# Strassen products of the GRU gates: the second and third of each seven added by TensorE in the PSUM bank of the first and fifth

## The chip, the cores and the metric

The kernel runs on one core of a Trainium2 chip. The metric is the device time of one launch in microseconds (us), as the median of the runs shown. TensorE (PE in the profile, with its weight loads listed apart as PEld), VectorE (DVE), ScalarE (ACT), GpSimd (POOL) and SyncE (SP) each run their own instructions in order and wait for each other by semaphores.

## The reference, cut to what matters

The first layer is a gated recurrent unit (GRU) over 128 graphs of 128 nodes and 256 channels. Its inputs are the normalised rows `h`, a convolution branch `x_conv` and a neighbour sum `x_nmp`; the change touches the gates only:

```python
x_in = jnp.concatenate([x_conv, x_nmp], axis=-1)
gi = x_in @ w_ih.T + b_ih
gh = x @ w_hh.T + b_hh
r = jax.nn.sigmoid(gi_r + gh_r)
z = jax.nn.sigmoid(gi_z + gh_z)
nn_ = jnp.tanh(gi_n + r * gh_n)
return (1.0 - z) * nn_ + z * x
```

Around it stand a layer norm with ReLU ahead of each layer and residual additions. The second layer is a grouped graph convolution on the first 25 nodes of each graph.

## The kernel before, in words

Everything is float32. The graphs are taken in 32 groups `q` of four. Two early stages (`stage_a`, `stage_b`, for two batches) do the convolution through a Fourier transform; `early(q)` computes the neighbour sums. The third stage begins at 720.4 us of the profiled execution. It runs `stage_c(q)` for every group, and beside it the second layer: `rows(q)` normalises the 32 rows that a group hands over, `prepare(blk)` and `block(blk)` work on 16 graphs at once.

The order of all instructions is made when the kernel is built, by `Order.run`. Each lane is a list of generators. A step of a generator ends with `yield cost, delay`: the cost is TensorE time, and is added to a clock; the generator may go on when the clock has passed its due time (the clock plus the delay). Among lanes that are due, the one with the least cost so far, divided by its weight, goes first. The lane of `stage_c` holds two groups at a time (`ahead=2`), and takes the one with the earlier due time. The lane of the second layer has weight 0.2, so it waits until the groups are not due, that is, at the yields with a delay of 0.2 between the products with `wn`.

In `stage_c(q)` three gate matrices are multiplied by Strassen's scheme, as seven products each over 2 x 2 blocks: `wrz` (reset gate `r` and update gate `z`, two output blocks of 128, six matmuls for each product), `wh` (one matmul for each) and `wn` (two). The operands are `hT`, `xm` and `xc`, and their block sums `th`, `tm` and `tc`, which DVE makes (`sums`, `some_sums`, line 552). With product indices 0 to 6 for the scheme's P1, P2, P3, P4, P5, P6, P7, an index below 3 uses a block of the plain operand and the others use a sum. A matmul of 128 x 256 appears in the profile as two records. Every product gets a PSUM bank from a pool: `pgat` has three banks (the products of `wrz` and `wn`), `ptmp` five (all else). A freed bank is handed out again in the order in which its last reader stands in the program; the next writer waits for that reader.

The order around the change, in a group: two products of the inverse transform (`pi`, line 673); the parts of products 0, 1 and 2 of `wrz` that need `hT` and `xm` only; in between `turn_back` (eight transposes `pc`, DVE line 690 and ACT line 693 make `xc`); then the parts that need `xc`. ACT copies product 0 to `u2` (line 740), DVE adds product 1 to it into `r1` (line 741), ACT copies product 2 to `r2` (line 745). DVE then builds the sums `u2`, `u3` for the other outputs (lines 761, 762, 769, 779, 780, 788), in the same way for `wh` in `va`, `vb`, `vt` (lines 760 to 797), and for `wn` in `r` itself (lines 805 to 823). Then come Tanh (line 825), three POOL operations for each half (lines 828 to 831, `d` and `z`), and, 11.0 of the builder's clock later, the eight transposes `po` (line 848) of the group before. The tiles `d` of a group's end have the same slots as `u2` and `u3` of the next group.

Of the kernel before, what the change touches and what calls it, by code (L numbers as in the profile page):

```python
# [10 lines left out]
AF = mybir.ActivationFunctionType  # L11
ALU = mybir.AluOpType
# [195 lines left out]
def kernel(ctx: ExitStack, tc: tile.TileContext, x, adj, consts, vecs, w_se, conv1_w,  # L208
                    conv2_w, w_msg, b_msg, w_ih, w_hh, W1, W2, b2, fusion_w, out):
    nc = tc.nc  # L210
# [7 lines left out]
    ptmp = ctx.enter_context(tc.tile_pool(name="ptmp", bufs=5, space=PSUM))  # L218
# [18 lines left out]
    def v(name, i=None):  # L237
        a, b = VAT[name]
        return vec[:, a:b] if i is None else vec[:, a + i:a + i + 1]
# [306 lines left out]
    def sums(name, q, x):  # L546


        t = LATE["co"].tile([P, 4, D], FP, tag=name, name=f"{name}{q}", bufs=1 + (name != "tc"))
        operands = ((0, x[:, 0, D:], x[:, 0, :D]), (1, x[:, 1, D:], t[:, 0]),  # L550
                    (2, x[:, 1, D:], x[:, 0, D:]), (3, t[:, 1], x[:, 1, :D]))
        return t, [lambda i=i, a=a, b=b: nc.vector.tensor_sub(t[:, i], a, b)  # L552
                   for i, a, b in operands]

    def some_sums(q, n):

        if q in IN:
            if q not in SUMS:
                hT, xm = IN[q]
                (th, a), (tm, b) = sums("th", q, hT), sums("tm", q, xm)  # L560
                SUMS[q] = th, tm, a + b
            while SUMS[q][2] and n != 0:
                SUMS[q][2].pop(0)()
                n = n and n - 1
# [92 lines left out]
    def stage_c(q):  # L657
# [11 lines left out]
        for h in range(2):  # L669
            yt = IN2.pop((q, h))  # L670
            pi = ptmp.tile([P, 2, D], FP, tag="tmp", name=f"pi{q}_{h}")
            for b in range(2):
                nc.tensor.matmul(pi[b * 64:(b + 1) * 64], inv[:F], yt[:, b::2],  # L673
                                 start=True, stop=True)
# [5 lines left out]
        def turn_back():  # L680

            for h in range(2):
                s = slice(h * D, (h + 1) * D)
                pc = ptmp.tile([P, 2, D], FP, tag="tmp", name=f"pc{q}_{h}")
                for co in range(2):
                    for i in range(2):
                        nc.tensor.transpose(pc[:, co, i * P:(i + 1) * P],  # L687
                                            xi[:, 2 * h + i, co * P:(co + 1) * P], ident)
                for co in range(2):
                    nc.vector.scalar_tensor_tensor(xc[:, co, s], pc[:, co],  # L690
                                                   scl["bn2"][:, co:co + 1], hT[:, co, s],
                                                   op0=ALU.mult, op1=ALU.add)
                    nc.scalar.activation(xc[:, co, s], xc[:, co, s], AF.Relu,
                                         bias=sft["bn2"][:, co:co + 1])

        wrz, wn, wh = LATE["wrz"], LATE["wn"], LATE["wh"]

        def factor(i, x, t):

            return ((x[:, 0, :D], x[:, 1, :D], x[:, 1, D:])[i] if i < 3  # L700
                    else t[:, (3, 0, 1, 2)[i - 3]])

        def part(ps, w, i, xs, first, last):


            n = [(m, o) for o in xs for m in range(w.shape[3] // P)]
            for j, (m, (k, x, t)) in enumerate(n):
                nc.tensor.matmul(ps[:, m], w[:, i, k, m * P:(m + 1) * P], factor(i, x, t),  # L708
                                 start=first and j == 0, stop=last and j == len(n) - 1)

        def product(w, i, xs, pool=pgat):
            ps = bank(w, i, pool)
            part(ps, w, i, xs, True, True)
            return ps

        def bank(w, i, pool=pgat):
            return pool.tile([P, w.shape[3] // P, D], FP, tag="gat" if pool is pgat else "tmp",
                             name=f"p{w.shape[3]}{q}_{i}")

        def sigmoid(dst, src, b):  # L720
            for m in range(2):
                nc.scalar.activation(dst[:, m], src[:, m], AF.Sigmoid, bias=brz[:, b + m:b + m + 1])  # L722

        xs = [(0, hT, None), (2, xm, None), (1, xc, None)]
        r = fr.tile([P, 2, 512], FP, tag="r", name=f"r{q}")
        u2 = fr.tile([P, 2, D], FP, tag="u2", name=f"u2{q}")
        u3 = fr.tile([P, 2, D], FP, tag="u3", name=f"u3{q}")
        r1, r2 = r[:, :, :D], r[:, :, D:]  # L730
        ps = [bank(wrz, i) for i in range(3)]
        for i in range(3):
            part(ps[i], wrz, i, xs[:2], True, False)
            yield 1.75, 0.0
            if i == 0:
                turn_back()
                yield 0.9, 0.0
        for i in range(2):
            part(ps[i], wrz, i, xs[2:], False, True)
        nc.scalar.activation(u2, ps[0], AF.Copy)  # L740
        nc.vector.tensor_tensor(r1, u2, ps[1], ALU.add)
        sigmoid(r1, r1, 0)
        yield 1.75, 0.0
        part(ps[2], wrz, 2, xs[2:], False, True)
        nc.scalar.activation(r2, ps[2], AF.Copy)
        tcs, todo = sums("tc", q, xc)
        for operation in todo:
            operation()
# [1 line left out]
        xs, xh = [(0, hT, th), (2, xm, tm), (1, xc, tcs)], [(0, hT, th)]  # L750

        ve = fr.tile([P, 3, 1, D], FP, tag="ve", name=f"ve{q}")
        va, vb, vt = ve[:, 0], ve[:, 1], ve[:, 2]
        r11, r12, r21, r22 = r[:, 0:1, :D], r[:, 0:1, D:], r[:, 1:2, :D], r[:, 1:2, D:]

        def gate(dst, src, row):
            nc.vector.scalar_tensor_tensor(dst, src, v("b_hh", 4 + row), dst,
                                           op0=ALU.add, op1=ALU.mult)

        nc.scalar.activation(va, product(wh, 0, xh, ptmp), AF.Copy)  # L760
        nc.vector.tensor_tensor(u2, u2, product(wrz, 5, xs), ALU.add)
        nc.vector.tensor_add(r2, r2, u2)
        yield 3.03, 0.0
        nc.vector.tensor_tensor(vt, va, product(wh, 1, xh, ptmp), ALU.add)
        gate(r11, vt, 0)
        nc.vector.tensor_tensor(va, va, product(wh, 5, xh, ptmp), ALU.add)
        yield 0.87, 0.0
        p5 = product(wrz, 4, xs)
        nc.vector.tensor_tensor(r2, r2, p5, ALU.add)  # L769
        sigmoid(r2, r2, 0)  # L770
        some_sums(q + 1, 2)
        yield 2.6, 0.0
        nc.vector.tensor_tensor(vb, va, product(wh, 6, xh, ptmp), ALU.add)
        yield 0.43, 0.0
        while q and q - 1 not in C_DONE:
            yield 0.0, 0.5
        z = fr.tile([P, 2, 512], FP, tag="z", name=f"z{q}")
# [1 line left out]
        nc.vector.tensor_tensor(u3, u2, product(wrz, 6, xs), ALU.add)  # L779
        nc.vector.tensor_tensor(z2, u3, p5, ALU.add)  # L780
        sigmoid(z2, z2, 2)
        some_sums(q + 1, 2)
        nc.vector.tensor_tensor(vt, vb, product(wh, 3, xh, ptmp), ALU.add)
        gate(r21, vt, 1)
        yield 3.03, 0.0
        xt = fr.tile([P, 4, D], FP, tag="xt", name=f"xt{q}")
        load_x(xt, q)
        nc.vector.tensor_tensor(z1, u3, product(wrz, 3, xs), ALU.add)
        sigmoid(z1, z1, 2)
        some_sums(q + 1, 2)  # L790
        yield 2.6, 0.0
        h5 = product(wh, 4, xh, ptmp)
        nc.vector.tensor_tensor(vb, vb, h5, ALU.add)
        gate(r22, vb, 1)
        nc.vector.tensor_tensor(va, va, h5, ALU.add)  # L795
        nc.vector.tensor_tensor(va, va, product(wh, 2, xh, ptmp), ALU.add)
        gate(r12, va, 0)
        some_sums(q + 1, 2)
        yield 0.87, 0.0

        xs = [(1, xm, tm), (0, xc, tcs)]
        u2 = fr.tile([P, 2, D], FP, tag="u2", name=f"v2{q}")
        u3 = fr.tile([P, 1, D], FP, tag="u3", name=f"v3{q}")
        v1, v2 = u2[:, 0:1], u2[:, 1:2]
        nc.scalar.activation(v1, product(wn, 0, xs), AF.Copy)
        yield 0.87, 0.2
        nc.vector.tensor_tensor(v2, v1, product(wn, 5, xs), ALU.add)
        nc.vector.tensor_add(r12, r12, v2)
        yield 0.87, 0.2
        p5 = product(wn, 4, xs)  # L810
        nc.vector.tensor_tensor(r12, r12, p5, ALU.add)
        yield 0.87, 0.2
        nc.vector.tensor_tensor(u3, v2, product(wn, 6, xs), ALU.add)
        nc.vector.tensor_add(r22, r22, u3)
        nc.vector.tensor_tensor(r22, r22, p5, ALU.add)
        nc.vector.tensor_add(r21, r21, u3)
        nc.vector.tensor_add(r11, r11, v1)
        yield 0.87, 0.2
        nc.vector.tensor_tensor(r21, r21, product(wn, 3, xs), ALU.add)
        yield 0.87, 0.2  # L820
        nc.vector.tensor_tensor(r11, r11, product(wn, 1, xs), ALU.add)
        yield 0.87, 0.2
        nc.vector.tensor_tensor(r12, r12, product(wn, 2, xs), ALU.add)
        for dc in (1, 0):
            nc.scalar.activation(r[:, dc], r[:, dc], AF.Tanh, bias=v("b_ih", 4 + dc))  # L825

# [276 lines left out]
    for bat, (during_a, during_b) in enumerate(((0.66, 0.5), (0.2, 0.65))):  # L1103
# [12 lines left out]
        tc.tile_pool(name="co", bufs=1, side="right", reuse_waits="tile"))  # L1116
    loads = Lane([stage_n(q) for q in range(NQ)])
    groups = Lane([stage_c(q) for q in range(NQ)], ahead=2)
    second = [setup_1()] + [part(blk) for blk in range(NBLK) for part in (prepare, block)]
    beside.weight = 0.5  # L1120
# [43 lines left out]
```

## Time and profile before

| | |
|---|---|
| median of 5 runs | 2127.11 us (2125.21 to 2132.17) |
| the profiled execution's own time | 2127.27 us |
| its span, first to last instruction | 2125.5 us |
| PE busy | 2052.5 us (97%) |
| DVE busy | 1240.2 us (58%), 2999 instructions |
| ACT busy | 699.9 us (33%) |
| POOL busy | 724.1 us (34%) |
| third stage, 720.4 to 2030.0 us | 1309.60 us, PE busy 1289.57, DVE 798.71, ACT 411.05 |

Durations of single instructions are means over their group in the profile. A record of a matmul ends when its result is modelled to be complete, so neighbouring records overlap; the distance from start to start is what a matmul takes from the engine. Idle time of PE is time in which no record is open.

### The profile page before, as it was taken

The page shows a single profiled execution, that of the slowest core. Times are in us where ns is not written, and L with a number is a line of the kernel's source. Part 1 is how long each engine was busy: PE and PEld are TensorE (multiplying, and loading weights), DVE is VectorE, ACT ScalarE, POOL GpSimd, SP SyncE. Part 2 cuts the span into 40 slices and gives each one's busy share as a digit, 9 for nine tenths or more (in the row PEclk, how much of TensorE's full clock was granted, in tenths as well). Part 3 has the DMA queues.
Part 4 walks back from the last instruction along what each step waited for, and adds up shares of the span by engine and source line. Part 5 has one row for each costly group of instructions (what it writes and reads, how often), then busy time and mean ns, then how long its engine had stood idle before and what let it go on. Part 6 is the DMA issues. An engine that isn't in the chain of part 4 may idle for free.

```text
span 2125.5 us, 31227 instructions
## 1 busy us (share of the span) xinstructions
PE 2052.5 (97%) x11316; PEld 1664.8 (78%) x11316; DVE 1240.2 (58%) x2999; ACT 699.9 (33%) x1575; POOL 724.1 (34%) x900
## 2 busy tenths in 40 slices
PE   6999999999999999999999999999999999999998
PEld 4667888788888777788778878878887887878875
DVE  5665444776544566756654655675565655665642
ACT  3554222344222343323233332233233223323333
POOL 2443665231566123512323233223323323233230
PEclk9999999999999999999999999999999999999999
DMA  9997778744777534222223222223232233223121
GB/s 179 267 266 231 259 256 264 207 142 148 260 259 257 180 109 153 67 92 61 76 70 102 77 79 84 77 75 85 71 99 73 78 92 91 78 80 101 26 78 50
DMA packets 187052, 281.68 MB, mean 133 GB/s; under 512 B 20685, under 2 KB 140242, under 8 KB 186898
## 3 DMA queue, kind: packets, MB, share of 16 engines
q1 hardware_dynamic: 156066, 184.81, 30.5%
q0 software_dynamic: 30000, 94.13, 13.9%
q8 instruction: 90, 1.47, 0.3%
q10 hardware_dynamic: 832, 0.74, 0.2%
q14 instruction: 64, 0.52, 0.1%
HBM read 187.34 MB, written 92.27 MB: 132 GB/s over the span
## 4 chain that ended last, share of the span: by engine, by line
PE 83%; DVE 8%; DMA 4%; ACT 1%; issue 1%; POOL 1%; SPq 0%; ACTq 0%; DVEq 0%; POOLq 0%
PE p L708 36%; PE pa L501 7%; PE pm L600 5%; PE ph L1024 5%; PE pz L1033 5%; PE pc L397 4%; PE pb L501 3%; PE pi L673 3%; PE px L626 3%; PE pf L408 2%; DMA wfd<-ws 2%; PE pg L1067 1%; PE po L848 1%; PE pc L687 1%; PE py L1007 1%
## 5 line engine op out<-in xcount | busy, mean ns | idle before, releaser
L828 POOL TENSOR_TENSOR d<-hTc,r 128x512 f32<-128x512 f32 x64 | 82.3, 1286 | 318.7 <-ACT r L825 308.3
L857 POOL DMA_DIRECT2D out<-xt x128 | 71.8, 567 | 263.1 <-DVE xt L854 259.0
L501 PE MATMUL pa<-wf,X 128*128 128x256 f32 x640 | 152.4, 381 | 0.0
L524 DVE SCALAR_TENSOR_TENSOR y<-pa,kk 128x512 f32<-128x512 f32 x78 | 53.8, 690 | 147.4 <-ACT kk L523 147.4
L722 ACT ACTIVATE r<-r,brz 128x256 f32<-128x256 f32 x128 | 58.1, 500 | 226.2 <-DVE r L769 198.5
L708 PE MATMUL p<-th,wrz 128*128 128x256 f32 x512 | 131.5, 379 | 0.7 <-ACT u L740 0.7
L708 PE MATMUL p<-tc,wrz 128*128 128x256 f32 x512 | 131.5, 379 | 0.4 <-DVE tc L552 0.4
L708 PE MATMUL p<-tm,wrz 128*128 128x256 f32 x512 | 131.4, 379 | 0.0
L501 PEld LDWEIGHTS pa<-wf,X 128*128 128x128 f32 x640 | 118.1, 190 | 16.4 <-issue 2.2
L397 PE MATMUL pc<-c1w,hTa 128*128 128x256 f32 x512 | 123.2, 387 | 3.7 <-ACT ef L588 2.3
L600 PE MATMUL pm<-wmsg,hT 128*128 128x256 f32 x512 | 123.9, 388 | 0.0
L690 DVE SCALAR_TENSOR_TENSOR xc<-pc,s_bn,hTc 128x256 f32<-128x256 f32 x128 | 53.1, 477 | 115.6 <-PE pc L687 115.6
L1024 PE MATMUL ph<-yz,w 128*128 128x96 f32 (+3 forms) x640 | 114.8, 334 | 4.0 <-DVE ve L795 2.7
L1024 PEld LDWEIGHTS ph<-yz,w 128*128 128x128 f32 x640 | 92.7, 202 | 26.0 <-issue 14.9
L397 PEld LDWEIGHTS pc<-c1w,hTa 128*128 128x128 f32 x512 | 94.4, 192 | 22.0 <-DVE h L400 4.0
L600 PEld LDWEIGHTS pm<-wmsg,hT 128*128 128x128 f32 x512 | 97.6, 194 | 16.5 <-issue 1.8
L1033 PE MATMUL pz<-hh,w 128*128 128x96 f32 (+3 forms) x640 | 108.5, 322 | 0.8 <-ACT hh L1026 0.8
L708 PEld LDWEIGHTS p<-th,wrz 128*128 128x128 f32 x512 | 97.2, 190 | 14.3 <-ACT u L740 1.1
L708 PEld LDWEIGHTS p<-tc,wrz 128*128 128x128 f32 x512 | 97.2, 190 | 14.0 <-DVE tc L552 0.8
L708 PEld LDWEIGHTS p<-tm,wrz 128*128 128x128 f32 x512 | 97.3, 190 | 13.2
L722 ACT ACTIVATE z<-z,brz 128x256 f32<-128x256 f32 x128 | 58.1, 501 | 145.8 <-DVE z L780 90.9
L1033 PEld LDWEIGHTS pz<-hh,w 128*128 128x128 f32 x640 | 87.2, 192 | 19.3 <-ACT hh L1026 1.5
(209 smaller groups left out, 4669.2 us busy)
## 6 DMA issues: line engine op xcount, KB each, us to landing
wf<-wfd SPq DMA_DIRECT2D x160, 256.0 KB, 3.6
wfd<-ws POOLq DMA_DIRECT2D x64, 320.0 KB, 7.2
yd<-y POOLq DMA_DIRECT2D x80, 256.0 KB, 3.5
yt<-yd SPq DMA_DIRECT2D x64, 320.0 KB, 4.5
w<-in_W SPq DMA_DIRECT2D x40, 512.0 KB, 3.6
xa<-in_x SPq DMA_DIRECT2D x128, 128.0 KB, 5.3
hTd<-hTa POOLq DMA_DIRECT2D x32, 512.0 KB, 4.6
hT<-hTd SPq DMA_DIRECT2D x32, 512.0 KB
```

What stands on the lines that cost most here:

```text
L397: nc.tensor.matmul(pc[:, i], hT[:, k, (2 * h + i) * N:(2 * h + i + 1) * N], c1w[:, k], start=(k == 0), stop=(k == 1))
L501: nc.tensor.matmul(ps, xk(k), WF[f][:, k, s], start=(k == 0), stop=(k == 1))
L524: nc.vector.scalar_tensor_tensor(y, pa, 2.0, kk[:, None].to_broadcast([P, 2, D]), op0=ALU.mult, op1=ALU.subtract)
L600: nc.tensor.matmul(pm[:, i], hT[:, k, j * N:(j + 1) * N], LATE["wmsg"][:, k], start=(k == 0), stop=(k == 1))
L626: nc.tensor.matmul(px[:, dc, i], msgs[h][:, i, dc * P:(dc + 1) * P], aT[:, 2 * h + i], start=True, stop=True)
L673: nc.tensor.matmul(pi[b * 64:(b + 1) * 64], inv[:F], yt[:, b::2], start=True, stop=True)
L708: nc.tensor.matmul(ps[:, m], w[:, i, k, m * P:(m + 1) * P], factor(i, x, t), start=first and j == 0, stop=last and j == len(n) - 1)
L722: nc.scalar.activation(dst[:, m], src[:, m], AF.Sigmoid, bias=brz[:, b + m:b + m + 1])
L828: nc.gpsimd.tensor_sub(d, hT[:, dc], r[:, dc])
L857: nc.gpsimd.dma_start(out=out[q * GB + j, WIDE:].rearrange("(t n) c -> n t c", n=WIDE), in_=xt[j * WIDE:(j + 1) * WIDE, 1:4])
L1024: nc.tensor.matmul(ph, w1[:, k, m * P:(m + 1) * P], yz[:, k, :, o:o + n], start=(k == 0), stop=(k == 1))
L1033: nc.tensor.matmul(pz, w2[:, g, m, cc * P:(cc + 1) * P], hs[g][:, m], start=(m == 0), stop=(m == 3))
```

## The change

The weights and the 63 matmuls of a group stay. What changes is where they add up, and when:

- The parts that need `hT` and `xm` only are now those of products 0, 5 and 4 of `wrz` (banks `p1`, `p6`, `p5`), not 0, 1 and 2.
- Product 1 of `wrz` is added by TensorE into bank `p1` after ACT has copied product 0 out of it to `u2`; the sigmoid of `r1` reads the bank. Product 2 is added into `p5` after DVE has read product 4 from it for `z2`; one DVE addition then gives `r2`. The copy of line 745 goes.
- The same for `wh` (product 1 into `h1` after the copy to `va`, product 2 into `h5` after DVE's addition to `vb`) and for `wn` (product 1 into `n1` after the copy to `v1`, product 2 into the bank of product 4).
- Two products of `wh` and two of `wn` and `wrz` no longer ask for a bank. The additions to `r12` and `r22` become one of twice the width.
- The order of the products, of the additions of the next group's sums and of some yields changes with it. `skip_group_check` is an argument for the builder's check of groups alone.

```diff
-        def part(ps, w, i, xs, first, last):
+        def part(ps, w, i, xs, first, last, again=False):
...
                                  start=first and j == 0, stop=last and j == len(n) - 1,
+                                 skip_group_check=again)
...
-        ps = [bank(wrz, i) for i in range(3)]
-        for i in range(3):
-            part(ps[i], wrz, i, xs[:2], True, False)
+        early = [(0, hT, th), (2, xm, tm)]
+        p1, p6, p5 = bank(wrz, 0), bank(wrz, 5), bank(wrz, 4)
+        for ps, i in ((p1, 0), (p6, 5), (p5, 4)):
+            part(ps, wrz, i, early, True, False)
             yield 1.75, 0.0
             if i == 0:
                 turn_back()
                 yield 0.9, 0.0
-        for i in range(2):
-            part(ps[i], wrz, i, xs[2:], False, True)
-        nc.scalar.activation(u2, ps[0], AF.Copy)
-        nc.vector.tensor_tensor(r1, u2, ps[1], ALU.add)
-        sigmoid(r1, r1, 0)
-        yield 1.75, 0.0
-        part(ps[2], wrz, 2, xs[2:], False, True)
-        nc.scalar.activation(r2, ps[2], AF.Copy)
+        part(p1, wrz, 0, xs[2:], False, True)
+        nc.scalar.activation(u2, p1, AF.Copy)
         tcs, todo = sums("tc", q, xc)
         for operation in todo:
             operation()
         yield 0.87, 0.0
...
-        nc.scalar.activation(va, product(wh, 0, xh, ptmp), AF.Copy)
-        nc.vector.tensor_tensor(u2, u2, product(wrz, 5, xs), ALU.add)
-        nc.vector.tensor_add(r2, r2, u2)
-        yield 3.03, 0.0
-        nc.vector.tensor_tensor(vt, va, product(wh, 1, xh, ptmp), ALU.add)
-        gate(r11, vt, 0)
+        h1 = bank(wh, 0, ptmp)
+        part(h1, wh, 0, xh, True, True)
+        nc.scalar.activation(va, h1, AF.Copy)
+        yield 0.43, 0.0
+        part(p1, wrz, 1, xs, False, True, True)
+        sigmoid(r1, p1, 0)
+        yield 2.6, 0.0
+        part(p6, wrz, 5, xs[2:], False, True)
+        nc.vector.tensor_tensor(u2, u2, p6, ALU.add)
+        part(h1, wh, 1, xh, False, True, True)
+        gate(r11, h1, 0)
+        yield 1.3, 0.0
+        part(p5, wrz, 4, xs[2:], False, True)
         nc.vector.tensor_tensor(va, va, product(wh, 5, xh, ptmp), ALU.add)
-        yield 0.87, 0.0
-        p5 = product(wrz, 4, xs)
-        nc.vector.tensor_tensor(r2, r2, p5, ALU.add)
-        sigmoid(r2, r2, 0)
         some_sums(q + 1, 2)
-        yield 2.6, 0.0
-        nc.vector.tensor_tensor(vb, va, product(wh, 6, xh, ptmp), ALU.add)
-        yield 0.43, 0.0
+        yield 1.3, 0.0
         while q and q - 1 not in C_DONE:
             yield 0.0, 0.5
...
         nc.vector.tensor_tensor(u3, u2, product(wrz, 6, xs), ALU.add)
         nc.vector.tensor_tensor(z2, u3, p5, ALU.add)
         sigmoid(z2, z2, 2)
+        nc.vector.tensor_tensor(vb, va, product(wh, 6, xh, ptmp), ALU.add)
         some_sums(q + 1, 2)
-        nc.vector.tensor_tensor(vt, vb, product(wh, 3, xh, ptmp), ALU.add)
-        gate(r21, vt, 1)
         yield 3.03, 0.0
         xt = fr.tile([P, 4, D], FP, tag="xt", name=f"xt{q}")
         load_x(xt, q)
         nc.vector.tensor_tensor(z1, u3, product(wrz, 3, xs), ALU.add)
         sigmoid(z1, z1, 2)
+        nc.vector.tensor_tensor(vt, vb, product(wh, 3, xh, ptmp), ALU.add)
+        gate(r21, vt, 1)
         some_sums(q + 1, 2)
-        yield 2.6, 0.0
-        h5 = product(wh, 4, xh, ptmp)
+        yield 3.03, 0.0
+        part(p5, wrz, 2, xs, False, True, True)
+        nc.vector.tensor_tensor(r2, u2, p5, ALU.add)
+        sigmoid(r2, r2, 0)
+        h5 = bank(wh, 4, ptmp)
+        part(h5, wh, 4, xh, True, True)
         nc.vector.tensor_tensor(vb, vb, h5, ALU.add)
-        gate(r22, vb, 1)
-        nc.vector.tensor_tensor(va, va, h5, ALU.add)
-        nc.vector.tensor_tensor(va, va, product(wh, 2, xh, ptmp), ALU.add)
-        gate(r12, va, 0)
-        some_sums(q + 1, 2)
-        yield 0.87, 0.0
+        yield 3.03, 0.0
...
-        v1, v2 = u2[:, 0:1], u2[:, 1:2]
-        nc.scalar.activation(v1, product(wn, 0, xs), AF.Copy)
+        v1, v2, v3 = u3, u2[:, 0:1], u2[:, 1:2]
+        n1 = bank(wn, 0)
+        part(n1, wn, 0, xs, True, True)
+        nc.scalar.activation(v1, n1, AF.Copy)
+        part(h5, wh, 2, xh, False, True, True)
+        nc.vector.tensor_tensor(va, va, h5, ALU.add)
+        yield 1.3, 0.2
+        nc.vector.tensor_tensor(v2, v1, product(wn, 5, xs), ALU.add)
+        gate(r22, vb, 1)
+        gate(r12, va, 0)
+        some_sums(q + 1, 2)
         yield 0.87, 0.2
-        nc.vector.tensor_tensor(v2, v1, product(wn, 5, xs), ALU.add)
-        nc.vector.tensor_add(r12, r12, v2)
+        part(n1, wn, 1, xs, False, True, True)
+        nc.vector.tensor_tensor(r11, r11, n1, ALU.add)
         yield 0.87, 0.2
-        p5 = product(wn, 4, xs)
-        nc.vector.tensor_tensor(r12, r12, p5, ALU.add)
+        nc.vector.tensor_tensor(v3, v2, product(wn, 6, xs), ALU.add)
+        nc.vector.tensor_tensor(r2, r2, u2, ALU.add)
+        nc.vector.tensor_add(r21, r21, v3)
         yield 0.87, 0.2
-        nc.vector.tensor_tensor(u3, v2, product(wn, 6, xs), ALU.add)
-        nc.vector.tensor_add(r22, r22, u3)
+        p5 = bank(wn, 4)
+        part(p5, wn, 4, xs, True, True)
         nc.vector.tensor_tensor(r22, r22, p5, ALU.add)
-        nc.vector.tensor_add(r21, r21, u3)
-        nc.vector.tensor_add(r11, r11, v1)
         yield 0.87, 0.2
         nc.vector.tensor_tensor(r21, r21, product(wn, 3, xs), ALU.add)
         yield 0.87, 0.2
-        nc.vector.tensor_tensor(r11, r11, product(wn, 1, xs), ALU.add)
-        yield 0.87, 0.2
-        nc.vector.tensor_tensor(r12, r12, product(wn, 2, xs), ALU.add)
+        part(p5, wn, 2, xs, False, True, True)
+        nc.vector.tensor_tensor(r12, r12, p5, ALU.add)
         for dc in (1, 0):
             nc.scalar.activation(r[:, dc], r[:, dc], AF.Tanh, bias=v("b_ih", 4 + dc))
```

More of the change, by code (lines that the diff above doesn't have):

```diff
@@ L708, in part @@
                 nc.tensor.matmul(ps[:, m], w[:, i, k, m * P:(m + 1) * P], factor(i, x, t),
-                                 start=first and j == 0, stop=last and j == len(n) - 1)
+                                 start=first and j == 0, stop=last and j == len(n) - 1,
+                                 skip_group_check=again)
         def product(w, i, xs, pool=pgat):
```

## The prediction

> **What bounds the kernel now.** I read the page first, then the waits of PE alone, then the third stage's window, and last the order of time around the lines that change. The page says that matmuls fill the span and that the chain which ended last is mostly theirs:
>
> ```profile
> PE 2052.5 (97%) x11316; PEld 1664.8 (78%) x11316; DVE 1240.2 (58%) x2999; ACT 699.9 (33%) x1575; POOL 724.1 (34%) x900
> ...
> PE 83%; DVE 8%; DMA 4%; ACT 1%; issue 1%; POOL 1%; SPq 0%; ACTq 0%; DVEq 0%; POOLq 0%
> ```
>
> The change lies in the third stage only. Its window (columns: stretch, length, PE, PEld, DVE, ACT, POOL busy, clock, DMA share, GB/s) leaves PE 1309.60 - 1289.57 = 20.0 us idle. DVE is busy for 61% there, ACT for 31%.
>
> ```profile
> 720.40:2030.00 1309.60, 1289.57 (x6594) 1042.94 (x6590) 798.71 (x1946) 411.05 (x900) 381.30 (x448) 0.99 0.30 83
> ```
>
> So whatever is taken from DVE and ACT can win about 20 us at most, and every new wait of PE costs its full length. PE's own waits (total us, times, longest) show what there is to win:
>
> ```profile
> PE py L1007 <- ACT x1h L929: 7.1, 3, 5.2
> ...
> PE p L708 <- DVE v L807: 3.7, 5, 0.8
> PE ph L1024 <- DVE ve L795: 2.7, 5, 0.9
> ...
> PE p L708 <- ACT u L740: 0.7, 1, 0.7
> PE p L708 <- DVE tc L552: 0.4, 1, 0.4
> ```
>
> The order of time in one group, around the copy to `u2`:
>
> ```profile
> 1202.82 2.75 PE L708 MATMUL p<-xc,wrz 128*128 128x256 f32 x12
> 1203.95 0.60 ACT L740 ACTIVATE u<-p 128x512 f32<-128x512 f32 x1 [2.59 <-PE p L708]
> 1204.81 0.69 DVE L741 TENSOR_TENSOR r<-u,p 128x512 f32<-128x512 f32 x1 [4.01 <-ACT u L740]
> 1205.41 0.59 PE L708 MATMUL p<-hTc,wh 128*128 128x256 f32 x2
> 1205.84 1.03 PE L708 MATMUL p<-th,wrz 128*128 128x256 f32 x4
> ```
>
> Twelve records take 1205.41 - 1202.82 = 2.59 us: 0.216 each, 0.432 for a matmul, 0.865 for a product's part of two. The first four belong to product 0 and have streamed in at 1203.685; ACT starts 0.265 later and needs 0.597 (mean of its row). The bank's next user, at 1205.84, has 1.73 (products 1 and 2) + 0.43 (the `wh` product) of cover. Where that cover fails, PE stands still. Once, where ACT came late because POOL's `z` held the slot of `u2`:
>
> ```profile
> 1076.25 0.59 PE L708 MATMUL p<-hTc,wh 128*128 128x256 f32 x2
> 1076.91 0.60 ACT L740 ACTIVATE u<-p 128x512 f32<-128x512 f32 x1 [4.71 <-POOL z L831]
> 1077.56 1.13 PE L708 MATMUL p<-th,wrz 128*128 128x256 f32 x4 [0.71 <-ACT u L740]
> ```
>
> The copy ends at 1077.51 and the matmul starts 0.05 later; its four records take 1.13 instead of 1.03, so a restart costs 0.10 more.
>
> **The change part by part**, for one of 32 groups.
>
> *Removed from DVE*: lines 741 (688 ns), 762 (694), 764 (411), 795 (414), which is 2.21 us; in the `wn` part the additions of 811 (419) and 817 (418), and 808 and 814 (425 each) become one of 512 columns (694 by the row of 762): 0.99. Together 3.20 us, 102 us over all groups; from ACT line 745, 575 ns, 18.4 us. None of it is the bound. 63 matmuls a group remain, at the same pitch, so PE's work is unchanged: 0. DVE and sigmoid instructions that now read PSUM are costed at their rows: line 795 takes 414 ns from PSUM, line 808 425 ns from SBUF.
>
> *What that relieves.* PE's waits for a late DVE in these lines are 3.7 (`v`) + 0.4 (line 813) + 2.7 (`ve`) + 0.4 (`tc`) = 7.2 us idle in 13 places. A wait also hides 0.16 us under the modelled tail of the record before (379 ns a record against 216 a pitch), 2.1 in all. Of `py`'s 7.1 I count 1.9: the wait of 5.2 stands behind POOL's preparation of the second layer, which stays. Gain 11.2 us; bounds 3 (the backlog only moves on to the next bank) and 20 (all the idle time of the stage).
>
> *Bank `p1`: a new wait for ACT.* Product 1 now goes into the bank that the copy to `u2` reads. Between them stands one `wh` matmul. From the end of product 0's stream: 0.265 + 0.597 + 0.05 = 0.912 until PE may start, 0.432 of cover, 0.48 of waiting, and 0.10 for the restart: 0.58 to 0.59, and x 32 = 19.0 us. Is there other work to fill it? The two yields on the way have no delay, and from 950 us on the second layer's steps stand at the `wn` yields alone, where the delay is 0.2. The transposes `po` are due 11.0 after the group before; the costs up to there are 1.72 + 1.75 + 0.9 + 1.75 + 1.75 + 0.87 + 0.43 = 9.17, so they come after product 1 (11.77), too late. The operations queued behind PE's wait are everything: PE is in order.
>
> Here rules bear on the row. The row says 0.265 us from the last streamed column to ACT's start. The Trainium skill, "TensorE: Matmul & The Clock Gate", section "Single matmul latency", gives a warm matmul a constant of 166 ns beyond its columns, the part that a stream hides; the trace agrees for the record (379 - 216 = 163 ns). With that alone the wait would be 0.166 + 0.597 + 0.05 - 0.432 = 0.38 and 12.2 us without the restart; with the row it is 19.0. I take the row, since it contains the hand-over to ACT. A second rule speaks against the change: "PSUM — Partial Sum Buffer", section "PSUM bank collisions raise a hardware error", asks to guard by bank and not by address. So the first matmul waits for the whole copy, not for its half of the columns; by address it would be 0.30 less, 9.4 us. No run here shows a wait for half a bank; 9 is my low end, 19 the value.
>
> *Bank `h5`: a new wait for DVE.* Product 2 of `wh` waits for DVE's addition to `vb`. From the end of product 2 of `wrz`: DVE starts 0.205 later (line 761 after its product: 1208.64 against 1208.43), makes `r2` (0.69) and `vb` (0.41), and 0.05 on: 1.36. PE has 0.43 + 0.865 = 1.30 of cover. Short by 0.06, plus 0.10 for the restart: 0.16, 5.2 us. DVE must be on time for that: from the end of `wrz` product 6, PE streams 14 matmuls (6.05 us), and DVE does 0.69 + 0.69 + 0.41 + 0.84 + 0.75 (the rows of the second layer) + 0.68 + 0.41 + 0.48 + 0.84 = 5.8. A slack of a quarter us. Bounds: 0, and 0.35 a group when rows work falls wrongly, 11 us.
>
> *Other reused banks.* `h1` has 2.6 us and more behind its copy; `p5` is read for `z2` 1.6 us after product 6 and needed after 3.5; `n1` has a whole product and a second-layer step behind its copy. Each 0, covered by those products. Which bank does `n1` take? Banks go out in the order of their last readers, as here, where the line-813 bank is given before the line-815 bank that was asked for earlier:
>
> ```profile
> 881.01 0.70 PE L708 MATMUL p<-xm,wn 128*128 128x256 f32 x2 [0.19 <-DVE v L813]
> ...
> 881.92 0.30 PEld L708 LDWEIGHTS p<-xm,wn 128*128 128x128 f32 x2 [0.18 <-DVE r L815]
> ```
>
> So `n1` gets the bank of product 6, free for 3 us: 0. Were it that of `p5`, it would wait for `r2`: 0.62 a group, 20 us.
>
> *POOL and the queues.* The slot of `u2` is also that of POOL's last `d`; in the group above POOL ends at 1203.27, 0.68 before the copy. Tanh of the first half now stands behind the last but one `wn` product instead of the last but two, a shift that ACT's other work already hides in most groups. Where the copy is late (1076.91), 1.73 us of cover are gone: 1.8 us once. The four `xt` loads on SP, the out transfers on POOL and `po` keep their order; `po` moves ahead by about 1 us, with POOL done 4 us before: 0. The `tc` sums, until now finished 0.6 us before PE needs them (1206.96 and 1207.57), come 4 us early.
>
> **Sum**: 19.0 + 5.2 + 1.8 - 11.2 = +14.8 us. Against the profiled execution's own 2127.27 that is 2142; the median, 2127.11, is 0.2 below it. A measurement of this kernel tells about 0.2% (4.3 us) from no change.
>
> **The rivals.** *Faster: `po` fills the wait.* If the eight transposes (0.87 us) land between the `wh` product and product 1, the 0.59 vanish in all groups: 5.2 + 1.8 - 11.2 = -4.2, and with a relief of 13 -6: 2121. It decides at a builder's clock of 11.0 against my 9.17. For it: a late start of a group shifts the sum. Against it: today `po` does not come at 10.49 either, only at 13.52, so the start is less than 0.51 late.
>
> *No change: DVE's backlog was worth more than I count.* All 20 us of idle time go, and `h5` never waits: 19.0 + 1.8 - 20 = +0.8, 2128. For it: DVE runs without a gap through the `wn` part. Against: waits on POOL's work and on ACT's `zt` are in the 20.
>
> *Much slower: DVE is late in `wn`.* Product 2 needs `r22`, and from the end of product 5 DVE has 4.6 us of work, PE 3.5 plus the second-layer steps. In groups with few of these up to 1.4 us are lost; with `h5` at its upper bound and a relief of 3: 19 + 11 + 1.8 - 3 = +29, 2156; with `n1` in the wrong bank 2162.
>
> **How the numbers follow.** My forecast has 0.68 (2133 with a relief of 20, 2150 with one of 3), the faster rival 0.13, no change 0.12, much slower 0.07. Slower by over 0.2% is 0.68 + 0.07 = 0.75. The range 2126 to 2154 leaves out the faster rival (0.13) and the far part of the last case (0.05).
>
> **What would show it.** Right: a PE wait on the copy to `u2` of about 0.3 to 0.5 us shown, some 30 times; a smaller one on `vb`; DVE near 1138 us; the waits on `v` and `ve` gone. Wrong: `po` between the `wh` product and product 1, no wait on `u2`, or PE idle no longer than before in the third stage.

## The result, and the profile after

The kernel after took 2123.34 us (median of 36 runs), the kernel before 2125.83 (71 runs): ratio 0.9988, 95% interval 0.9983 to 0.9993. That is 2.5 us faster, 1.5 to 3.6 by the interval, and less than the 0.2% that the prediction named as no change; some 2 of the 2.5 go with the granted clock (last section). The prediction, 2142 with a range from 2126, was wrong by 19 us.

The page of the kernel after, busy time and chain. PE's share of the chain has gone from 83 to 88%, DVE's from 8 to 3%:

```profile
PE 2057.4 (97%) x11316; PEld 1658.2 (78%) x11316; DVE 1176.0 (55%) x2775; ACT 686.9 (32%) x1543; POOL 723.2 (34%) x900
...
PE 88%; DMA 3%; DVE 3%; POOL 3%; ACT 2%; issue 1%; SPq 0%; POOLq 0%; DVEq 0%; ACTq 0%
```

The third stage (columns as before): PE is now idle for 1309.40 - 1295.89 = 13.5 us of it, where it was 20.0. DVE's busy time fell by 63 us:

```profile
720.60:2030.00 1309.40, 1295.89 (x6599) 1036.43 (x6600) 735.48 (x1724) 398.08 (x868) 379.28 (x448) 0.99 0.30 83
```

All that the gates' products wait for on PE (total us, times, longest). The wait on the copy is there 31 times, as the prediction said. The waits on `v`, `ve`, `tc` and, with them, on `x1h` have left the list:

```profile
PE p L708 <- ACT u L742: 10.0, 31, 0.4
...
PE p L708 <- DVE r L823: 2.4, 2, 1.8
...
PE p L708 <- ACT v L805: 0.5, 1, 0.5
```

The same place in the timeline of one group, after:

```profile
1197.57 1.33 POOL L836 TENSOR_TENSOR z<-d,r 128x512 f32<-128x512 f32 x1
1197.70 1.48 DVE L552 TENSOR_TENSOR tc<-xc 128x256 f32<-128x256 f32 x1
1197.75 1.03 PE L708 MATMUL p<-xc,wrz 128*128 128x256 f32 x4
1198.61 0.59 PE L708 MATMUL p<-hTc,wh 128*128 128x256 f32 x2
1198.93 0.60 ACT L742 ACTIVATE u<-p 128x512 f32<-128x512 f32 x1 [2.65 <-POOL z L836]
...
1199.58 1.13 PE L708 MATMUL p<-hTc,wrz 128*128 128x256 f32 x4 [0.37 <-ACT u L742]
...
1202.27 0.93 PE L853 MATMUL po<-cst,z 128*128 128x128 f32 x7
```

The `wh` matmul starts at 1198.61 and takes 0.43, so PE is free at 1199.04. Product 1 starts at 1199.58, 0.05 after the whole copy has ended (1198.93 + 0.60), and `po` stands behind product 1. From start to start the wait costs 0.54 us here, of which 0.37 are shown and the rest lies under the modelled tail of the record before. In five groups, of which this is one, the copy starts some 0.06 late because POOL's `z` (line 836) still holds the slot of `u2`; in most the wait costs 0.48, with 0.32 shown (10.0 over 31 in the list). Over 31 groups that makes 15.1 us, and with the restart (1.13 instead of 1.03 us, 0.10 each) 18.3.

The list shows one wait that the change brings and the prediction priced only in its rival "much slower": product 2 of `wn` waits for the addition to `r22` (line 823) in two early groups, 2.4 us in all.

So the cost of 18 to 19 us that the prediction put first is there in full, and something gave back 20 us or more where the prediction counted 11. The experiments ask what.

### The profile page after: what moved, and what is told of

Same layout as the page of the kernel before. It is cut to its first block, busy times and chain, and to the rows that moved or that the text cites. A ratio compares the mean times of both kernels' runs of the same rounds, so it can differ in the third digit from the quotient of the medians.

```text
span 2123.9 us, 30965 instructions
## 1 busy us (share of the span) xinstructions
PE 2057.4 (97%) x11316; PEld 1658.2 (78%) x11316; DVE 1176.0 (55%) x2775; ACT 686.9 (32%) x1543; POOL 723.2 (34%) x900
## 4 chain that ended last, share of the span: by engine, by line
PE 88%; DMA 3%; DVE 3%; POOL 3%; ACT 2%; issue 1%; SPq 0%; POOLq 0%; DVEq 0%; ACTq 0%
PE p L708 39%; PE pa L501 7%; PE ph L1029 5%; PE pz L1038 5%; PE pm L600 5%; PE pc L397 4%; PE pb L501 3%; PE pf L408 3%; PE px L626 2%; PE pi L673 2%; DMA wfd<-ws 2%; PE pg L1072 1%; PE po L853 1%; PE ph L386 1%; PE pc L687 1%
## 5 line engine op out<-in xcount | busy, mean ns | idle before, releaser
L708 PE MATMUL p<-hTc,wrz 128*128 128x256 f32 x384 | 106.1, 399 | 10.0 <-ACT u L742 10.0
L708 PEld LDWEIGHTS p<-hTc,wrz 128*128 128x128 f32 x384 | 68.3, 191 | 55.5 <-ACT u L742 22.5
L1031 ACT ACTIVATE hh<-ph,vec 128x96 f32<-128x96 f32 (+3 forms) x160 | 64.2, 402 | 140.0 <-PE ph L1029 130.8
L708 PEld LDWEIGHTS p<-tm,wrz 128*128 128x128 f32 x512 | 97.9, 191 | 13.5
```

The source lines that it names most:

```text
L1031: nc.scalar.activation(hh[:, m], ph, AF.Relu, bias=v("b1", g * 4 + m))
```

## The experiments

| run | kernel | median us | ratio to before, 95% interval |
|---|---|---|---|
| after | the change | 2123.34 | 0.9988 [0.9983, 0.9993] |
| e7_nocover | after, no cover for the copy | 2137.67 | 1.0068 [1.0049, 1.0086] |
| e1_cover1 | after, cover of two `wh` products in all | 2111.19 | 0.9935 [0.9922, 0.9948] |
| e2_cover2 | after, cover of three `wh` products in all | 2104.49 | 0.9905 [0.9890, 0.9919] |
| e9_cover2_h5 | e2, and more cover for `h5` | 2104.67 | 0.9897 [0.9880, 0.9914] |
| e3_before_less | before, all of the relief alone | 2115.22 | 0.9950 [0.9934, 0.9965] |
| e5_less_early | before, its early half | 2123.17 | 0.9987 [0.9976, 0.9999] |
| e4_less_late | before, its late half | 2110.99 | 0.9932 [0.9916, 0.9948] |
| e6_put_back | after, DVE's old load put back as scratch additions | 2130.51 | 1.0017 [1.0007, 1.0026] |
| e8_later_po | after, `po` due later | 2124.45 | 0.9999 [0.9985, 1.0013] |
| e10_put_back2 | e2, DVE's old load put back in the same way | 2110.54 | 0.9929 [0.9912, 0.9946] |
| e12_own_banks | e10, with own banks for products 1 and 2 of `wh` and `wn` | 2104.61 | 0.9898 [0.9882, 0.9915] |
| e13_late_order | before, the new order from `wh` product 4 on alone | 2106.85 | 0.9908 [0.9892, 0.9925] |

### What the wait for the copy costs

No cover: the `wh` product goes behind product 1.

```diff
         h1 = bank(wh, 0, ptmp)
-        part(h1, wh, 0, xh, True, True)
-        nc.scalar.activation(va, h1, AF.Copy)
-        yield 0.43, 0.0
         part(p1, wrz, 1, xs, False, True, True)
         sigmoid(r1, p1, 0)
         yield 2.6, 0.0
+        part(h1, wh, 0, xh, True, True)
+        nc.scalar.activation(va, h1, AF.Copy)
+        yield 0.43, 0.0
```

> The changed kernel, with product 0 of wh moved behind product 1 of wrz, so that nothing stands behind the copy to u2 and TensorE waits 0.43 us longer in each group. Theory A: 0.43 x 32 = 14 us above the changed kernel, near 2137. Rival B: under 5 us above it.

The ratio rises by 0.0080 against after, 17 us (13 to 21). The waits of PE:

```profile
PE p L708 <- ACT u L742: 23.4, 31, 0.8
```

23.4 - 10.0 = 13.4 us, which is 31 times the 0.432 of the matmul that no longer stands there: the wait is paid to its full length.

More cover: the `wh` products 5 (first run), and 5 and 6 (second), stand ahead of product 1. The second edit:

```diff
         nc.scalar.activation(va, h1, AF.Copy)
-        yield 0.43, 0.0
+        h6 = product(wh, 5, xh, ptmp)
+        h7 = product(wh, 6, xh, ptmp)
+        yield 1.3, 0.0
         part(p1, wrz, 1, xs, False, True, True)
         sigmoid(r1, p1, 0)
+        nc.vector.tensor_tensor(va, va, h6, ALU.add)
+        nc.vector.tensor_tensor(vb, va, h7, ALU.add)
```

> The changed kernel, with product 5 of wh moved ahead of the sum in p1: the copy to u2 has 0.865 us of TensorE work behind it instead of 0.432. Theory A (the wait for the copy costs its full length on the path, about 0.58 us in each of 31 groups, and the relief of VectorE has paid for it with about 20 us): 0.05 us of wait stays, 0.43 us a group go, 13 to 16 us below the changed kernel's 2123, near 2109. Rival B (the wait is absorbed, since TensorE would have waited for VectorE later anyway, and the relief is only about 11 us): within 3 us of 2123.

> As e1_cover1, with product 6 of wh moved ahead as well: 1.30 us of TensorE work behind the copy, which needs 0.912. Theory A: the wait and its restart are gone, 18 us below the changed kernel, near 2105. Rival B: within 3 us of 2123.

With 0.865 of cover against the 0.912 needed, one shown wait of 0.2 us is left and the ratio falls by 0.0053 (11 us); with 1.30 none is left and it falls by 0.0083 (17.6 us). The first is short of cover by 0.05 only, and still misses 6 us of the second's gain: 0.05 and a restart of 0.10 in 31 groups account for 4.6 of them. With the copy covered, the change is worth 20 us, and both runs, with less cover and with more, agree with the prediction's term for bank `p1`, 19.0.

### What the wait for `h5` costs

```diff
         nc.scalar.activation(v1, n1, AF.Copy)
+        yield 0.87, 0.2
         part(h5, wh, 2, xh, False, True, True)
         nc.vector.tensor_tensor(va, va, h5, ALU.add)
-        yield 1.3, 0.2
         nc.vector.tensor_tensor(v2, v1, product(wn, 5, xs), ALU.add)
...
-        yield 0.87, 0.2
+        yield 1.3, 0.2
```

> e2_cover2 with product 2 of wh moved behind product 5 of wn, so that the addition to vb has more TensorE work behind it. In the changed kernel this place shows no wait, but 0.083 us for the restart in 28 groups: 2.4 us below e2_cover2, near 2102. If the restart is not the bank's, no change; if the gates come too late by it, up to 5 us more.

The ratio differs from that of the run without this edit by 0.0008 (1.7 us), well inside both intervals, and the medians are the same: the gain of 2.4 us that was expected is not shown. The 2.4 itself is read from the trace of after: in 28 groups the first matmul into this bank takes 0.083 us more and no wait is shown. In these DVE's addition to `vb` ends 0.06 to 0.08 us before the matmul starts; in the other four it ends 0.5 us or more before, and the matmul takes no longer than others.

### What DVE's smaller load is worth

First the relief alone, in the kernel before: the additions that the change removes, and ACT's copy of line 745, are left out there, so some terms of the gates are missing (not every line of the edit is shown).

```diff
-        nc.vector.tensor_tensor(r1, u2, ps[1], ALU.add)
-        sigmoid(r1, r1, 0)
+        sigmoid(r1, ps[1], 0)
...
-        nc.vector.tensor_add(r2, r2, u2)
-        nc.vector.tensor_tensor(vt, va, product(wh, 1, xh, ptmp), ALU.add)
-        gate(r11, vt, 0)
+        gate(r11, product(wh, 1, xh, ptmp), 0)
...
-        nc.vector.tensor_tensor(va, va, h5, ALU.add)
...
-        nc.vector.tensor_add(r12, r12, v2)
...
-        nc.vector.tensor_tensor(r12, r12, p5, ALU.add)
...
-        nc.vector.tensor_add(r22, r22, u3)
+        nc.vector.tensor_tensor(r2, r2, u2, ALU.add)
...
-        nc.vector.tensor_add(r11, r11, v1)
```

> The kernel before, with the instructions that the change takes from VectorE and ScalarE left out (lines 741, 745, 762, 764, 795, 811, 817, and 808 with 814 as one of twice the width), so the gates lack those terms; no bank is used twice. It is the relief alone. Theory A: the third stage's idle time of 20 us goes nearly whole, 19 us or more below before, near 2106. Rival B: 11 us or less below before, 2115 or above.

> The kernel before with the early part of the relief alone: lines 741, 745, 762 and 764 left out (1.8 us of VectorE and 0.6 of ScalarE a group), so the gates lack those terms. If VectorE's backlog in the wn part is what TensorE waits for, work so far ahead of it matters little: under 3 us, 2122 or above. If the total of VectorE's work counts, 1.8 of 3.2 us, so 5 to 6 us of the 10, near 2119.

> The kernel before with DVE's additions of lines 795, 811 and 817 left out and those of 808 and 814 made one of 512 columns (some terms of the gates are missing): the late half of the relief alone, 1.65 us in a group, in the old order and with the old banks. With the early additions left out as well the ratio was 0.995 (about 2115), with the early ones alone 0.9987. If the waits come from DVE's backlog in the wh and wn part: 2114 to 2118, the waits on v L807 and ve gone, that of py on x1h still there. If both halves are needed: 2121 to 2126.

All of it is worth 0.0050 (10.6 us, 7 to 14 by the interval), close to the 11.2 of the prediction. The early half (lines 741, 762 and 764: 1.8 us of DVE's time in each group) is worth 0.0013 (2.8 us), and the stalls in its trace are those of before. The late half alone, 1.4 us in a group (0.41 + 0.99 of the prediction's working; the 1.65 of the expectation was too high), gives 0.0068 (14.5 us), more than expected; its interval overlaps that of the whole relief. So the late half does what the whole relief does, and the waits hang on the stretch from the last `wh` products to the first `wn` additions. What stays in the trace of the whole relief is the wait of `py`:

```profile
PE py L999 <- ACT x1h L921: 6.0, 3, 4.7
```

In after that wait is gone too. The relief alone, in the old order, therefore brings ten to fifteen of the twenty us, and not the whole.

Then the reverse: after, with six scratch additions (2 of 512 columns, 4 of 256) that give DVE its old load.

```diff
+        nc.vector.tensor_tensor(sc, u2, u2, ALU.add)
...
+        nc.vector.tensor_tensor(sc[:, 0:1], va, va, ALU.add)
...
+        nc.vector.tensor_tensor(sc[:, 0:1], v2, v2, ALU.add)
```

> The changed kernel with six additions into a scratch tile put back on VectorE near their old places (two of 512 columns, four of 256, about 3.05 us a group by the rows of before). Theory C (after e3_before_less: VectorE's relief is worth about 10 us, and about another 10 come from the new order and the banks that are no longer asked for): 8 to 12 us above the changed kernel, near 2133. Theory D (the relief is worth all 20, and e3_before_less came out low for another reason): near 2143. Theory E (with the new order the work no longer matters): within 3 us of 2123.

The ratio rises by 0.0029 (6 us), between what two of the expectations said, but the waits of before do not return: `v`, `ve` and `x1h` are absent from the list of PE's waits, and what the products wait for grows by 2.4 us in sum.

```profile
PE p L708 <- ACT u L742: 10.0, 31, 0.4
PE p L708 <- DVE r L830: 3.6, 3, 2.1
PE p L708 <- DVE r L821: 1.2, 3, 0.7
PE p L708 <- ACT v L810: 0.5, 1, 0.5
```

The rest of the 6 us is not in the waits; half of the 6 goes with a lower granted clock (last section). With the old load PE still doesn't wait as it did. Something else in the change can keep these waits away.

### The shared banks, or the order

Three things were left: rows handed to the second layer a step sooner, because `po` moved ahead; products that ask for no bank; and the new order of the steps. First `po`:

```diff
-        yield 0.87, 11.0
+        yield 0.87, 13.0
```

> The changed kernel with the due time of the transposes po at 13.0 instead of 11.0, so that they stand one step later, behind the completed bank p6, and with them the hand-over to rows(q) of the second layer. The copy's wait stays. Theory C: the wait of TensorE on x1h, 5.2 us in before and gone in the changed kernel, is a matter of where rows stand in VectorE's queue beside the preparation of the second layer; it comes back, about 5 us, near 2128. Rivals D and E: no change beyond 2 us.

The ratio is 0.0011 above that of after, and its interval holds both kernels. The wait for `x1h` near 1050 us doesn't come back; one of 5 us appears at the very end, where the last `po` (2078.43) is late and nothing else is left for PE:

```profile
2084.38 1.78 PE L1012 MATMUL py<-r,x1h 128*128 128x212 f32 x4 [4.96 <-ACT x1h L934]
```

That is more than what little this kernel lost, 2.3 us by the ratio, and the theory of the sooner `po` finds no support.

Then two kernels with the copy covered and DVE's old load. In the first that load is scratch additions, in the second `wh` and `wn` products 1 and 2 have banks of their own again, with the additions of before:

```diff
-        part(h5, wh, 2, xh, False, True, True)
+        h3 = product(wh, 2, xh, ptmp)
         nc.vector.tensor_tensor(va, va, h5, ALU.add)
+        nc.vector.tensor_tensor(va, va, h3, ALU.add)
...
-        part(n1, wn, 1, xs, False, True, True)
-        nc.vector.tensor_tensor(r11, r11, n1, ALU.add)
+        nc.vector.tensor_add(r11, r11, v1)
+        nc.vector.tensor_tensor(r11, r11, product(wn, 1, xs), ALU.add)
...
-        part(p5, wn, 2, xs, False, True, True)
+        n3 = product(wn, 2, xs)
         nc.vector.tensor_tensor(r12, r12, p5, ALU.add)
+        nc.vector.tensor_tensor(r12, r12, n3, ALU.add)
```

> The kernel after with two products of wh ahead of product 1, so that PE does not wait for the copy to u2, and with six scratch additions put back on DVE (2 of 512 columns, 4 of 256, about 3 us in a group, their results unused): DVE has its old amount of work, but the new order and the shared banks stay. The kernel with that cover alone took 2104.5. Theory order and banks: the waits of the kernel before went because of the new order and because products no longer ask for banks, not because DVE has less to do: 2106 to 2110, no waits on v, ve or r of over 3 us in sum. Theory relief: the 3 us of DVE work taken away are what removed the waits: about 10 us come back, 2114 to 2116, with waits of the products for the late additions.

> As the run beside it (cover of two wh products, DVE's amount of work as before), but products 1 and 2 of wh and of wn have banks of their own again and are added by DVE in four additions that replace four of the six scratch ones; products 1 and 2 of wrz stay in shared banks, with two scratch additions of 512 columns. So DVE's work and the order are those of the run beside it, and only the banks differ. If the order of the steps alone removed the waits: within 2 us of the run beside it. If the shared banks of wh and wn did: 4 to 12 us slower than it, with waits of products for v, ve or r at the places of the kernel before.

With own banks and the old load the time is 2104.61, the same as with shared banks and the small load (2104.49). Neither the relief nor the sharing in `wh` and `wn` is needed (`wrz` still shares its banks here). The run with scratch additions alone is 6 us slower, which neither expectation named. The two intervals just overlap; the traces show 1.7 us of it as longer waits on `r` (3.7 against 2.0), and one of the scratch additions (line 837) took 753 ns where its like (line 823) took 418. The rest stays open.

Last, the order alone. In the kernel before, only the steps from `wh` product 4 on, with their yields, are put in the order of the change. All 63 matmuls of a group, all of DVE's additions and a bank for every product are as before:

```diff
         nc.vector.tensor_tensor(vb, vb, h5, ALU.add)
-        gate(r22, vb, 1)
-        nc.vector.tensor_tensor(va, va, h5, ALU.add)
-        nc.vector.tensor_tensor(va, va, product(wh, 2, xh, ptmp), ALU.add)
-        gate(r12, va, 0)
-        some_sums(q + 1, 2)
-        yield 0.87, 0.0
+        yield 0.43, 0.0
...
         nc.scalar.activation(v1, product(wn, 0, xs), AF.Copy)
-        yield 0.87, 0.2
+        h3 = product(wh, 2, xh, ptmp)
+        nc.vector.tensor_tensor(va, va, h5, ALU.add)
+        nc.vector.tensor_tensor(va, va, h3, ALU.add)
+        yield 1.3, 0.2
         nc.vector.tensor_tensor(v2, v1, product(wn, 5, xs), ALU.add)
-        nc.vector.tensor_add(r12, r12, v2)
+        gate(r22, vb, 1)
+        gate(r12, va, 0)
+        some_sums(q + 1, 2)
         yield 0.87, 0.2
...
```

The other `wn` products follow in the order 1, 6, 4, 3, 2 instead of 4, 6, 3, 1, 2, each with its additions.

> The kernel before with the order of the change in the last part of a group alone: wn product 0, wh product 2 and a yield of 1.3 with delay 0.2; then wn 5 with the gates of r22 and r12 and two sums behind it; then wn 1, 6, 4, 3, 2. Every product has its own bank and every addition of the kernel before is made, so DVE has the same work; all that stands ahead of wh product 4 is as before. The run with the whole new order, the old amount of DVE work and own banks for wh and wn took 2104.6. Theory late order: the waits of the kernel before come from DVE's run of work ahead of wn (the gates of r22 and r12 and the sums between the last wh products and the first wn additions) and from the second layer's rows behind it; moved behind wn product 5 they hold nobody: 2104 to 2111, and PE's waits on v, ve and x1h gone. Theory whole order: the early part (parts of P6 and P5 first, P2 and P3 later) is needed too: 2114 to 2122, the waits on v and ve still there.

This gives 0.9908, 20 us less than before (16 to 23), with no other part of the change. In its trace DVE is as busy as before in the third stage (793 us, before 799), and PE is idle for 1309.30 - 1301.29 = 8.0 us of it, where before it was 20.0:

```profile
720.70:2030.00 1309.30, 1301.29 (x6681) 1051.52 (x6678) 793.22 (x1965) 421.36 (x915) 391.23 (x465) 0.99 0.30 84
```

Of the waits that the order bears on, these are left:

```profile
PE py L1009 <- ACT x1h L931: 4.4, 2, 3.4
...
PE p L708 <- DVE r L811: 0.6, 2, 0.3
...
PE ph L1026 <- DVE ve L802: 0.3, 1, 0.3
```

How the order does it is seen in the timeline of one place. Before, around a step of the second layer (`ph`, line 1024, and `pz`, line 1033):

```profile
1143.92 0.41 DVE L793 TENSOR_TENSOR ve<-ve,p 128x256 f32<-128x256 f32 x1
...
1144.44 0.48 DVE L757 SCALAR_TENSOR_TENSOR r<-ve,vec,r 128x256 f32<-128x256 f32 x1
1144.85 0.41 DVE L795 TENSOR_TENSOR ve<-ve,p 128x256 f32<-128x256 f32 x1
...
1145.40 0.66 PE L1024 MATMUL ph<-yz,w 128*128 128x96 f32 x4 [0.44 <-DVE ve L795]
...
1147.33 0.42 ACT L929 ACTIVATE x1h<-x1h 128x256 f32<-128x256 f32 x1 [2.91 <-DVE x1h L928]
1147.66 1.02 ACT L1026 ACTIVATE hh<-ph,vec 128x96 f32<-128x96 f32 x4
...
1148.03 1.15 PE L1033 MATMUL pz<-hh,w 128*128 128x112 f32 x8 [0.20 <-ACT hh L1026]
```

`ph` wants the bank of `h5`, whose last reader, line 795, stands on DVE behind a gate (line 757): 0.44 us. Another gate and two sums follow ahead of `x1h` (line 928), so ACT comes late to its half of `x1h`, and `hh` stands behind that: another 0.20. The order alone, at the like place:

```profile
1138.53 1.98 PE L1026 MATMUL ph<-yz,w 128*128 128x96 f32 x16
...
1138.96 0.42 DVE L793 TENSOR_TENSOR ve<-ve,p 128x256 f32<-128x256 f32 x1
...
1139.29 0.41 DVE L802 TENSOR_TENSOR ve<-ve,p 128x256 f32<-128x256 f32 x1
1139.81 0.42 DVE L803 TENSOR_TENSOR ve<-ve,p 128x256 f32<-128x256 f32 x1
1140.15 0.41 DVE L930 TENSOR_SCALAR x1h<-x,mv,rs 128x256 f32<-128x256 f32 x1
...
1141.51 0.42 DVE L805 TENSOR_TENSOR v<-v,p 128x256 f32<-128x256 f32 x1 [0.95 <-ACT hh L1028]
1141.85 0.87 DVE L757 SCALAR_TENSOR_TENSOR r<-ve,vec,r 128x256 f32<-128x256 f32 x2
```

The three additions that free banks stand together, `x1h` directly behind them, and the two gates and the sums, which nobody waits for here, come behind `v`. All 16 records of `ph` run without a break, and DVE even has a gap of 0.95 us ahead of `v`. The amount of its work is the same.

The fastest of these are the change with the copy covered (2104.49, and 2104.67 with `h5` covered too) and own banks (2104.61); they can't be told apart, and by the medians each is 19 us below after and 21 below before. The smallest edit of before that gets nearly there is the order alone.

## Why the prediction was wrong

*Bank `p1`, 19.0: right.* 18.3 us from start to start in the trace, 17.6 when covered, and its three parts (0.265 from the stream's end to ACT, 0.597, 0.05) hold: the trace of after has 0.26, 0.597 and 0.05 in most groups. PE waited for the whole copy: the rule of the Trainium skill that the prediction weighed, "PSUM — Partial Sum Buffer", section "PSUM bank collisions raise a hardware error", agrees with the 0.05 between the copy's end and the matmul's start, and the 9.4 of waiting for half a bank falls. `po` came after product 1, as worked out.

*Bank `h5`, 5.2: over-sized.* 2.4 by the trace; the wait of 0.06 didn't show and the restart was 0.083. *POOL's once, 1.8:* no wait of that length; the 0.06 in five groups came instead. Together some 4.5 us too much. *Left out: the bank of `wn` product 4*, whose wait for `r22` stood in a rival only: 2.4.

*"What that relieves", 11.2: the step that failed.* The new order and the relief together gave back 20 us or more, as the "no change" rival had it in total: it put +0.8 against the measured -2.5. Its reason, a backlog of DVE worth more than counted, is not what the runs show. As the worth of removed DVE work the 11.2 was nearly right (10.6). But the sum counted only instructions that the change removes. What the change moves went uncosted: the gates of `r22` and `r12` (0.48 each) and two sums (0.42 each), 1.8 us in a group, leave the stretch of DVE where additions that free banks stand, and the `wn` products come in another order. These moves alone are worth 20 us in the kernel before. The two gains don't add, since they remove the same waits: the own-banks run, with the new order and the old load, is as fast as the run with the small load.

The exclusion of `py`'s wait of 5.2 ("stands behind POOL's preparation") was right for part of it. Before, at that place:

```profile
1052.97 0.25 DVE L950 TENSOR_REDUCE dg<-b 25x16 f32<-25x96 f32 x1 [0.26 <-POOL b L945]
...
1056.10 0.41 DVE L928 TENSOR_SCALAR x1h<-x,mv,rs 128x256 f32<-128x256 f32 x1
...
1057.01 1.78 PE L1007 MATMUL py<-r,x1h 128*128 128x212 f32 x4 [5.21 <-ACT x1h L929]
```

Only the reductions of line 950 wait for POOL. Behind them, and ahead of `x1h`, come three additions, two gates and two sums. The order alone moves the gates and sums, and the wait there shrinks by 1.8 us, to the 3.4 in that run's list. In after the rest goes too: `x1h` stands ahead of the reductions (L955), and `py` doesn't wait. Why it comes ahead there was not separated.

```profile
1048.74 0.58 DVE L933 TENSOR_SCALAR x1h<-x,mv,rs 128x256 f32<-128x256 f32 x1
...
1049.24 1.28 DVE L955 TENSOR_REDUCE dg<-b 25x16 f32<-25x400 f32 x4
1050.28 0.88 PE L1012 MATMUL py<-r,x1h 128*128 128x212 f32 x4
```

The sum with the measured terms: after with the copy covered, which still pays for `h5` and `r22`, is 20.2 us below before, and the copy's wait is 18.3, so -1.9; measured is -2.5 (-1.5 to -3.6). The 20.2 is itself known to 17 to 23 only, so this closes within the noise. Which of the moved instructions counts most wasn't separated: gates, sums, the order of the `wn` products and the yields, which place the steps of the second layer, moved together.

*The signs.* The wait on the copy came, 31 times, and those on `v` and `ve` went. A wait on `vb` isn't shown, and DVE is busy for 1176.0 us, not near 1138: some of its sums took longer (last section).

## What to carry to other kernels

When an engine is 60% busy and still late, look at where its instructions stand before you count them: here those that free a bank belonged first, those that nobody waits for behind them. Removing 1.4 us of work in the stretch that mattered helped too; removing 1.8 us elsewhere did next to nothing. An edit's moved instructions want a price as much as its removed ones. Before letting PE add into a bank that another engine must first read out, count the work that stands between: 0.9 us were needed here, 0.43 were there, and the missing half microsecond came back 31 times.

## What was unexpected of the hardware

A matmul of 128 x 256 that starts right behind the addition or copy it must wait for took 0.083 to 0.104 us longer to its successor than one in a stream, even where no wait is shown.

DVE's sums `tc` (line 552) read no PSUM and took 0.42 us each before. In after many come while POOL works on `d` and `z`, as in the timeline above, and those that do are longer: 31 of one form took 0.94 us on average and 16 of another 1.30, the rest of these two forms still 0.42. That is some 30 us of DVE's time, and most of what is missing between the 102 us of additions removed and the fall by 64 in the page. PE didn't wait for it.

The granted clock of PE falls to 0.5 for stretches of 3.4 to 10 us, and records of 256 columns then stand 0.427 us apart instead of 0.216. One such stretch begins between 1047 and 1063 us in all traces but one (`po` due later); the others lie at different places. In the third stage of the profiled executions, up to the end of the span, they add up to between 18 and 37 us. Each costs half its length, except the last in every trace, which begins behind the last matmul. So two executions can differ by some 10 us for this reason alone; to see 5 us took the medians of several. Less half of this time, the third stage takes 1389.9 us before, 1388.7 after, 1372.3 with three `wh` products of cover, 1369.0 with own banks and 1372.7 with the order alone: nearly the ranking of the medians.

The medians hold some of the clock too. The mean granted clock of a run is 0.9875 on average in the kernel before and 0.9891 in after, and among the runs of before the time falls by 1.3 us for each 0.001 of it (correlation -0.85). By an estimate from these figures some 2 of the 2.5 us between before and after are the clock's, as are 2 of the 20 of the order alone, 3 of the 6 that the scratch additions cost in after (mean clock 0.9868), and 3 of the 4 between the late half of the relief (0.9900) and the whole (0.9878). At one clock, before and after can't be told apart. Whether a kernel's own work sets its clock isn't shown.
